# A two-layer graph convolution: the first twelve gathered chunks stand in tiles that the weights and row vectors take later

## The chip, the cores and the metric

The kernel runs on one core of one Trainium2 chip. The time is the device time of one execution, in microseconds (us); less is better. Three runs of the kernel before gave a median of 2044.03 us. Beside them one execution was profiled.

## What is computed

There are N = 6250 nodes with D = 512 values each and E = 100000 edges (src, dst), sorted by dst. All is in float32. A layer norm with a ReLU goes first, then two Chebyshev graph convolutions with a layer norm and a leaky ReLU between them, and at the end x is added:

```python
def _cheb_norm(src, dst, n):
    deg = segment_sum(ones(E), src, n)
    dinv = where(deg > 0, rsqrt(maximum(deg, 1.0)), 0.0)
    return -dinv[src] * dinv[dst]
def _cheb_conv(x, src, dst, norm, W0, W1, b):
    tx1 = segment_sum(x[src] * norm[:, None], dst, N)
    return x @ W0 + tx1 @ W1 + b

h = maximum(layernorm(x), 0.0)
g = _cheb_conv(h, src, dst, norm, W1_0, W1_1, b1)
g = layer_norm(g, gamma, beta)
g = where(g >= 0, g, 0.01 * g)
out = x + _cheb_conv(g, src, dst, norm, W2_0, W2_1, b2)
```

## The kernel before

**Chunks.** The sorted edges are cut into 782 chunks of 128 edges. For a chunk, one indirect DMA on GpSimd's queue gathers the 128 rows that its src name, 2 KB each, into one slot of 128 partitions x 512 values (256 KB). TensorE then multiplies the chunk by a selection matrix (`sel`, one column for each of 32 neighbouring dst) and adds it up into the rows of the nodes. Three chunks make a unit and four units a group: group 0 has chunks 0 to 2, group 1 chunks 3 to 14, group 2 chunks 15 to 26, and so on, 66 groups in each layer. `sums` (L621) does the matmuls of one group.

**Slots.** `places` is one tile with 63 slots. Slots 14 to 62 first hold the 49 blocks of x (128 nodes each). From these the normed table `tab[0]` is made and written to DRAM, and a slot that has been written out is taken by a gather. The last eight slots later hold layer 1's weights, so R = 55 slots are in turn for chunks: chunk t of layer 0 stands in slot t modulo 55 (`zr`), and chunk t can be gathered only when chunk t - 55 has been summed. `gather_to` issues the gathers of a group in order, ahead of the group's work, up to chunk 3 * unit[g] + 55.

**Raw chunks.** `tab[0]` is not complete when the first gathers are wanted. So the first RAW = 64 chunks of layer 0 are gathered from x itself ("raw"). Their norm is made good later: `find` and `look_up` fetch, four chunks at a time, the scale and shift of each gathered row by small matmuls (L477, L492), VectorE steps (L480, L495, L498, L501) and one ScalarE activation for each chunk (L503, a ReLU with scale and shift). Chunks from RAW on come from `tab[0]`, whose rows carry dinv in a further column, and `scale` (L610) multiplies the selection by it.

**First stage.** The first 14 raw chunks go into the slots that never held x. While VectorE builds one-hot matrices for the degrees (L340, 25 rounds), `make_table` norms blocks of x in place (L311), SyncE writes them to `tab[0]` (L312), and `gather_raw` (L236) gathers raw chunks into the slots that come free. The last entry for `tab[0]` is the column of dinv for its first 31 blocks (L393), elements of four bytes.

**Main loop.** `usual_path` writes out the order of TensorE, GpSimd and SyncE by hand: on each of them instructions run in written order, and one that waits holds all behind it. ScalarE's and VectorE's order is left to a scheduler. For each group g: gathers, look-ups, then for the blocks of nodes that are complete `turn` (own rows of h transposed, sums placed, L651), then `sums`, look-ups, and the dense products with the layer's weights `w_sb` (L532) and the layer norm. Block 0 is complete with group 2, so its products come in group 3.

**Weights and row vectors.** `w_sb` is two tiles of four 128 x 512 parts (1 MB each) for layer 0's W1_1 and W1_0. `bias1`, `bias2`, `gam` and `bet` are tiles of 128 x 512; each gets its vector as one row on partition 0 (L204), and `widen` (L798, L799) spreads it over all partitions by a matmul with ones and a VectorE copy. In the kernel before, `load_rest(1)` loads the row vectors in the first stage, `load_rest(3)` stands ahead of the main loop and loads the weights, and `widen` runs behind the sums of group 1. SyncE's written order of the first stage and that of the main loop are two chains that may be merged; in the trace the two weight loads (L201) stand among the first stage's table writes.

Of the kernel before, what the change touches and what calls it, by code (L numbers as in the profile page):

```python
# [12 lines left out]
OP = mybir.AluOpType  # L13
# [6 lines left out]
P = 128  # L20
# [4 lines left out]
Q = 32  # L25
NQ = P // Q
STEP = 3
DRIFT = 32
RE = 14
RAW = 64  # L30
PAD = 16
# [11 lines left out]
def gnn_kernel(  # L43
# [34 lines left out]
    N, D = x.shape  # L78
# [5 lines left out]
    KD = D // P  # L84
    NC = -(-E // P)
# [12 lines left out]
    def dup(ap, n):  # L98
# [4 lines left out]
    zero_row = (NB - LATE) * P  # L103
# [90 lines left out]
    def load_rest(k):  # L194
        if k < 3:
            load_x(*groups[6 + k])
        if k == 2:
            nc.sync.dma_start(tab[1][zero_row : zero_row + 1, :], places[P - 1 : P, RE + NB - 1, :D])
        if k == 3:
            for t, w in zip(w_sb, (W1_1, W1_0)):  # L200
                nc.sync.dma_start(t, w.rearrange("(k p) d -> p k d", p=P))  # L201
# [32 lines left out]
    def gather_raw(lo, hi):  # L234
        for t in range(lo, min(hi, R)):
            nc.gpsimd.indirect_dma_start(  # L236
                out=places[:, t, :D], out_offset=None, in_=x,
                in_offset=bass.IndirectOffsetOnAxis(ap=sidx[:, t : t + 1], axis=0))

    gather_raw(0, RE)  # L240

# [63 lines left out]
    def make_table(i0, n):  # L305

        for lo in range(i0, i0 + n, 2):
            hi = min(lo + 2, i0 + n)
            for i in range(lo, hi):
                v = places[:, RE + i, :D]  # L310
                nc.scalar.activation(v, v, AF.Relu, bias=nb_all[:, i : i + 1], scale=rs_all[:, i : i + 1])  # L311
# [96 lines left out]
def usual_path(tc, have):  # L408
    nc = tc.nc
    (x, out, tab, h_tab, ndinv, sidx, dlx, iota_r, w_sb, W2_1, W2_0, w_late, ident, eps, ones, first, nodes_ps, node_of, minus,  # L410
     unsorted, dinv, sdinv, bias1, bias2, gam, bet, unseen, unit, N, E, D, NB, NC, NU, NS, KD, rows, places, R,
     load_rest, sc, pick, src_lo, src_hi, eidx, e_src, zero_row, p_id) = (
        have[n] for n in ("x out tab h_tab ndinv sidx dlx iota_r w_sb W2_1 W2_0 w_late ident eps ones first nodes_ps node_of "
                          "minus unsorted dinv sdinv bias1 bias2 gam bet unseen unit N E D NB NC NU NS KD rows places "
                          "R load_rest sc pick src_lo src_hi eidx e_src zero_row p_id").split())
    AHEAD = 2
# [10 lines left out]
    with ExitStack() as es:  # L427
        pool = es.enter_context(tc.tile_pool(name="main", bufs=2))
        psum = es.enter_context(tc.tile_pool(name="main_ps", bufs=2, space=bass.MemoryType.PSUM))
        es.enter_context(tc.manual_schedule(engines={PE, POOL, SP}))  # L430
        is_lo, found, looked, gathered = [], 0, 0, R
        behind, behind_rows, summed = {}, {}, {}
# [4 lines left out]
        def zr(layer, t):  # L437
            return places[:, (layer * NC + t) % R, :D]

        def gather_to(layer, end):  # L440
            nonlocal gathered
            for t in range(gathered, min(end, NC)):
                own_scale = layer == 0 and t >= RAW
                nc.gpsimd.indirect_dma_start(  # L444
                    out=places[:, t % R, :] if own_scale else zr(layer, t), out_offset=None,
                    in_=x if layer == 0 and t < RAW else tab[layer],
                    in_offset=bass.IndirectOffsetOnAxis(
                        ap=lidx[:, t - SHIFTED : t - SHIFTED + 1] if layer and t >= SHIFTED else sidx[:, t : t + 1], axis=0))
            gathered = max(gathered, min(end, NC))
# [149 lines left out]
        def scale(sel, chunk, of=(0, NQ)):  # L599

            at = chunk[0][0]
            start = chunk[of[0]][0]
            end = chunk[min(of[1], len(chunk)) - 1][-1] + 1
            if end <= RAW:
                return
            each = sel.rearrange("p q s e -> p (q s) e")
            cut = sorted({start, end} | {t for t in range(start, end) if t % R == 0})
            for lo, hi in zip(cut, cut[1:]):
                v = each[:, lo - at : hi - at, :]
                last = nc.vector.tensor_tensor(  # L610
                    v, v, places[:, lo % R : lo % R + hi - lo, D : D + 1].to_broadcast([P, hi - lo, Q]), op=OP.mult)
            return last
# [173 lines left out]
        find("ps")  # L786
        load_rest(3)
        for i in range(AHEAD):
# [12 lines left out]
        for layer in range(2):  # L801
# [5 lines left out]
            for g in range(NS):  # L807
# [408 lines left out]
```

## Time and profile before

| | |
|---|---|
| median of 3 runs | 2044.03 us (2043.89 to 2047.14) |
| the profiled execution | 2042.93 us, of which its span is 2041.0 us |
| mean granted TensorE clock | 0.916 |
| TensorE busy | 1678.5 us (82%) |
| GpSimd busy | 1506.2 us (74%), 1564 gathers among its instructions |
| VectorE, ScalarE busy | 703.4 us (34%), 406.3 us (20%) |
| moved by DMA | 527.46 MB, mean 258 GB/s |

In the rows of the profile PE is TensorE, DVE VectorE, ACT ScalarE, POOL GpSimd, SPq SyncE's queue. A row in order of time has the start, the duration, the engine, the line, the operation, and in brackets the idle time before it and what ended that. A row of a stretch has for PE, PE's weight loads, DVE, ACT and POOL the busy time and the number of instructions, then the granted clock, the share of the DMA engines and GB/s. A group's row has its count, the busy time and the mean ns of one, and the engine's idle time ahead of its members. TensorE's busy time is not TensorE at its peak, since matmuls are pipelined.

### The profile page before, as it was taken

What the parts mean: (1) busy time and instruction counts of PE and PEld (TensorE: products, weight loads), DVE (VectorE), ACT (ScalarE), POOL (GpSimd) and SP (SyncE); (2) the same over time, 40 slices, a digit from 0 to 9 for tenths busy, and PEclk for the clock granted to TensorE, in tenths of its full rate; (3) what the DMA queues carried; (4) which work ended last, traced back from release to release, by engine and by line L of the source; (5) the groups of instructions that cost most, each with busy time, mean ns of one, the idle gap of its engine ahead of it and who ended that gap; (6) DMA issues with size and microseconds to landing.
All of it is one profiled execution on the core that took longest, in us unless ns stands there. A gap on an engine that the chain in (4) does not pass through costs nothing.

```text
span 2041.0 us, 19914 instructions
## 1 busy us (share of the span) xinstructions
PE 1678.5 (82%) x6838; PEld 662.6 (32%) x6838; DVE 703.4 (34%) x1483; ACT 406.3 (20%) x740; POOL 1506.2 (74%) x1578
## 2 busy tenths in 40 slices
PE   5579997778787767877889888888888888888887
PEld 4444432223333222333333332323332223333332
DVE  7975443232453333443462212122121212212221
ACT  7794221111211111221210101001010001011110
POOL 4677777777777777777777777777777777777774
PEclk9879998889988888988999988999998999999999
DMA  9998888888888888888887888887788888878875
GB/s 338 377 313 255 277 263 248 258 243 262 279 276 256 254 249 252 263 260 260 248 258 234 251 251 251 246 253 246 245 257 251 245 248 256 246 247 256 271 236 157
DMA packets 189414, 527.46 MB, mean 258 GB/s; under 512 B 34550, under 2 KB 36112, under 8 KB 189304
## 3 DMA queue, kind: packets, MB, share of 16 engines
q0 software_dynamic: 125120, 415.98, 68.0%
q1 hardware_dynamic: 64184, 110.12, 15.0%
q8 instruction: 56, 0.92, 0.2%
q14 instruction: 54, 0.44, 0.1%
HBM read 474.31 MB, written 51.66 MB: 258 GB/s over the span
## 4 chain that ended last, share of the span: by engine, by line
PE 42%; DMA 27%; POOL 14%; issue 11%; DVE 6%; ACT 1%; POOLq 0%; DVEq 0%; ACTq 0%; SPq 0%
DMA places<-tab,sidx 21%; PE u_ps L532 16%; POOL places L444 14%; PE ps L621 12%; PE an_ps L651 7%; DMA places<-tab,lidx 6%; PE hT_ps L711 1%; PE hT_ps L520 1%; DVE hi L340 1%; DVE lo L340 1%; PE hT_ps L492 1%; DVE st L671 0%; DVE sel L610 0%; PE both_ps L354 0%; DVE st L385 0%
## 5 line engine op out<-in xcount | busy, mean ns | idle before, releaser
L444 POOL DMA_INDIRECT places<-tab,sidx x1206 | 1145.0, 949 | 372.6 <-issue 266.2
L621 PE MATMUL ps<-places,sel 128*32 128x512 f32 x3128 | 531.6, 688 | 153.6 <-DMA places<-tab,sidx 84.9
L651 PE MATMUL an_ps<-agg,there 128*128 128x512 f32 (+1 forms) x580 | 281.6, 618 | 102.6 <-ACT agg L631 98.1
L444 POOL DMA_INDIRECT places<-tab,lidx x270 | 255.3, 945 | 82.3 <-issue 60.3
L621 PEld LDWEIGHTS ps<-places,sel 128*32 128x32 f32 x3128 | 106.3, 119 | 548.1 <-issue 196.5
L571 DVE TENSOR_TENSOR sel<-dlx,nodes_ps 128x384 f32<-128x384 f32 (+3 forms) x134 | 72.3, 541 | 424.8 <-PE ps L621 424.6
L631 ACT ACTIVATE agg<-ps 128x512 f32<-128x512 f32 (+1 forms) x132 | 78.4, 594 | 576.0 <-PE ps L621 553.6
L532 PE MATMUL u_ps<-w,hT 128*128 128x512 f32 (+1 forms) x392 | 178.7, 599 | 13.1 <-ACT hT L522 13.1
L651 PEld LDWEIGHTS an_ps<-agg,there 128*128 128x128 f32 (+1 forms) x580 | 108.9, 197 | 227.4 <-ACT agg L631 117.0
L532 PE MATMUL u_ps<-w,aT 128*128 128x512 f32 (+1 forms) x392 | 178.4, 598 | 2.5 <-DVE aT L713 2.5
L532 PE MATMUL u_ps<-places,hT 128*128 128x512 f32 (+1 forms) x392 | 176.9, 594 | 2.2 <-ACT hT L522 2.2
L532 PE MATMUL u_ps<-places,aT 128*128 128x512 f32 (+1 forms) x392 | 176.6, 593 | 1.5 <-DVE aT L713 1.5
L610 DVE TENSOR_TENSOR sel<-sel,places 128x384 f32<-128x384 f32 (+11 forms) x73 | 35.3, 485 | 375.1 <-DMA places<-tab,sidx 367.6
L662 DVE TENSOR_TENSOR u_ps<-u_ps,bias 128x512 f32<-128x512 f32 x46 | 32.2, 700 | 286.3 <-PE u_ps L532 286.3
L522 ACT ACTIVATE hT<-hT_ps 128x512 f32<-128x512 f32 (+1 forms) x98 | 58.2, 594 | 277.3 <-PE hT_ps L520 276.7
L639 DVE TENSOR_SCALAR there<-iota_r,node_of 128x128 f32<-128x128 f32 (+1 forms) x290 | 86.5, 301 | 60.9 <-PE an_ps L651 58.3
L704 ACT ACTIVATE an<-an_ps,ndinv 128x512 f32<-128x512 f32 (+1 forms) x98 | 67.1, 684 | 201.7 <-PE an_ps L651 201.4
L674 ACT ACTIVATE sd<-mv,eps 128x1 f32<-128x1 f32 (+1 forms) x49 | 14.4, 294 | 464.3 <-DVE mv L672 464.3
L236 POOL DMA_INDIRECT places<-in_x_dram,sidx x55 | 70.3, 1278 | 46.6 <-ACT junk L291 10.9
L532 PEld LDWEIGHTS u_ps<-w,aT 128*128 128x128 f32 (+1 forms) x392 | 72.5, 191 | 85.7 <-issue 79.4
L532 PEld LDWEIGHTS u_ps<-places,aT 128*128 128x128 f32 (+1 forms) x392 | 72.1, 190 | 83.1 <-issue 80.5
L532 PEld LDWEIGHTS u_ps<-w,hT 128*128 128x128 f32 (+1 forms) x392 | 71.3, 192 | 85.4 <-issue 71.7
(166 smaller groups left out, 1255.1 us busy)
## 6 DMA issues: line engine op xcount, KB each, us to landing
places<-tab,sidx POOLq DMA_INDIRECT x1206, 3.9
h_tab<-g SPq DMA_DIRECT2D x48, 256.0 KB, 5.8
xt<-in_x_dram SPq DMA_DIRECT2D x48, 256.0 KB, 5.1
out_dram<-t SPq DMA_DIRECT2D x48, 256.0 KB, 3.7
h<-tab SPq DMA_DIRECT2D x46, 256.0 KB, 5.0
tab<-t SPq DMA_DIRECT2D x46, 256.0 KB, 4.0
h<-h_tab SPq DMA_DIRECT2D x46, 256.0 KB, 4.5
tab<-places SPq DMA_DIRECT2D x22, 528.0 KB, 10.1
```

The lines of the kernel that those rows point to most:

```text
L236: nc.gpsimd.indirect_dma_start(out=places[:, t, :D], out_offset=None, in_=x, in_offset=bass.IndirectOffsetOnAxis(ap=sidx[:, t : t + 1], ax ...
L340: nc.vector.tensor_tensor(t, s[:, g * 2 * GJ : (g + 1) * 2 * GJ].rearrange("p (j s) -> p j s", s=2)[:, :, None, :] .to_broadcast([EP, GJ, ...
L444: nc.gpsimd.indirect_dma_start(out=places[:, t % R, :] if own_scale else zr(layer, t), out_offset=None, in_=x if layer == 0 and t < RAW el ...
L522: nc.scalar.activation(hT[:, :, :r], ps[:, :, :r], AF.Copy)
L532: nc.tensor.matmul(u_ps[:r], hT[:, kc, :r], w[:, kc, :], start=(start and kc == 0), stop=(stop and kc == KD - 1))
L571: nc.vector.tensor_tensor(sel[:, q : q + k, :w, :], of, node[:, q : q + k, None, :].to_broadcast([P, k, w, Q]), op=OP.is_equal)
L610: last = nc.vector.tensor_tensor(v, v, places[:, lo % R : lo % R + hi - lo, D : D + 1].to_broadcast([P, hi - lo, Q]), op=OP.mult)
L621: nc.tensor.matmul(ps[q * Q : (q + 1) * Q, :], sel[:, q, s, :], zr(layer, chunk[q][s]), start=(s == 0), stop=(s == len(chunk[q]) - 1 and ( ...
L631: nc.scalar.activation(agg[g][: n * Q], ps[: n * Q], AF.Copy)
L639: behind[1] = nc.vector.tensor_scalar(t[:m, :r], iota_r[:m, :r], node_of[:m, g : g + 1], -(1.0 + i * P), op0=OP.subtract, op1=OP.is_equal)
L651: nc.tensor.matmul(placed[i][:r], t[:m, :r], agg[g][:m, :], start=(g == inside[i][0]), stop=(g == inside[i][-1]))
L704: nc.scalar.activation(an[:r], placed.pop(i)[:r], AF.Copy, scale=ndinv[:r, i : i + 1])
```

## The change

Twelve slots more are found in tiles that lie empty at the start: the eight parts of `w_sb` and the four tiles of the row vectors (`lent`, X = 12). Chunks 0 to 11 are gathered there, straight behind each other at the start, and the 14 free slots of `places` take chunks 12 to 25. All further raw gathers move up by twelve chunks. A chunk t from 12 on stands in slot (t - 12) modulo 55. RAW grows from 64 to 76, so three more groups of four chunks are looked up, and `scale` begins with chunk 76. The weights and the row vectors are loaded by `load_rest(3)` behind the sums of group 1, which end the use of the lent tiles, and `widen` moves from behind group 1's sums to behind group 2's. The bound of `gather_to` (3 * unit[g] + 55) stays as it was.

```diff
-RAW = 64
+RAW = 76
...
+    lent = [t[:, k, :] for t in w_sb for k in range(KD)] + [bias1, bias2, gam, bet]
+    X = len(lent)
...
     def load_rest(k):
         if k == 3:
             for t, w in zip(w_sb, (W1_1, W1_0)):
                 nc.sync.dma_start(t, w.rearrange("(k p) d -> p k d", p=P))
-        if k == 1:
             for t, v in ((bias1, b1), (bias2, b2), (gam, gamma), (bet, beta)):
                 nc.sync.dma_start(t[0:1], dup(v, 1))
...
     def gather_raw(lo, hi):
-        for t in range(lo, min(hi, R)):
+        for t in range(lo, min(hi, X + R)):
             nc.gpsimd.indirect_dma_start(
-                out=places[:, t, :D], out_offset=None, in_=x,
+                out=lent[t] if t < X else places[:, t - X, :D], out_offset=None, in_=x,
...
-    gather_raw(0, RE)
+    gather_raw(0, X + RE)
...
-            gather_raw(RE + lo, RE + hi)
+            gather_raw(X + RE + lo, X + RE + hi)
...
-        is_lo, found, looked, gathered = [], 0, 0, R
+        is_lo, found, looked, gathered = [], 0, 0, X + R
...
         def zr(layer, t):
-            return places[:, (layer * NC + t) % R, :D]
+            k = layer * NC + t
+            return lent[k] if k < X else places[:, (k - X) % R, :D]
...
-            cut = sorted({start, end} | {t for t in range(start, end) if t % R == 0})
+            cut = sorted({start, end} | {t for t in range(start, end) if (t - X) % R == 0})
...
         find("ps")
         find("ps")
-        load_rest(3)
         for i in range(AHEAD):
             load(0, i)
...
                 sums(layer, g, sel, chunk, count_late(sel, chunk) if layer == 1 else None, of)
                 if layer == 0 and g == 1:
+                    assert STEP * unit[g + 1] >= X
+                    load_rest(3)
+                if layer == 0 and g == 2:
                     widen()
```

More of the change, by code (lines that the diff above doesn't have):

```diff
@@ L411, in usual_path @@
      unsorted, dinv, sdinv, bias1, bias2, gam, bet, unseen, unit, N, E, D, NB, NC, NU, NS, KD, rows, places, R,
-     load_rest, sc, pick, src_lo, src_hi, eidx, e_src, zero_row, p_id) = (
+     load_rest, sc, pick, src_lo, src_hi, eidx, e_src, zero_row, p_id, lent, X) = (
         have[n] for n in ("x out tab h_tab ndinv sidx dlx iota_r w_sb W2_1 W2_0 w_late ident eps ones first nodes_ps node_of "
                           "minus unsorted dinv sdinv bias1 bias2 gam bet unseen unit N E D NB NC NU NS KD rows places "
-                          "R load_rest sc pick src_lo src_hi eidx e_src zero_row p_id").split())
+                          "R load_rest sc pick src_lo src_hi eidx e_src zero_row p_id lent X").split())
     AHEAD = 2
@@ L444, in gather_to @@
                 nc.gpsimd.indirect_dma_start(
-                    out=places[:, t % R, :] if own_scale else zr(layer, t), out_offset=None,
+                    out=places[:, (t - X) % R, :] if own_scale else zr(layer, t), out_offset=None,
                     in_=x if layer == 0 and t < RAW else tab[layer],
```

3 lines of the change are left out of this document (2 added, 1 removed).

## The prediction

> **What bounds the kernel now.** I read the page first (span, busy shares, groups), then busy time by stretch, then GpSimd's and TensorE's instructions in order of time between 8 and 205 us, last SyncE's issues. The page's span, and the group that issues most gathers:
>
> ```profile
> span 2041.0 us, 19914 instructions
> L444 POOL DMA_INDIRECT places<-tab,sidx x1206 | 1145.0, 949 | 372.6 <-issue 266.2
> L621 PE MATMUL ps<-places,sel 128*32 128x512 f32 x3128 | 531.6, 688 | 153.6 <-DMA places<-tab,sidx 84.9
> ```
>
> One gather takes GpSimd 0.949 us and about 0.3 us pass before the next (372.6 over 1206). The sums (L621) mostly wait for gathers when they wait. Busy time by stretch, the columns and one stretch of 200 us:
>
> ```profile
> core 0: us, PE busy (x) PEld busy (x) DVE busy (x) ACT busy (x) POOL busy (x), PEclk, DMA share, GB/s
> 1200.00:1400.00 200.00, 172.79 (x620) 61.41 (x619) 40.68 (x88) 20.62 (x33) 151.26 (x161) 0.93 0.81 250
> ```
>
> 161 gathers in 200 us are one every 1.25 us without a pause, while TensorE has 14% to spare: the queue of gathers sets the pace. GpSimd in order of time (start, duration, and in brackets what it waited for):
>
> ```profile
> 29.19 2.54 POOL L236 DMA_INDIRECT places<-in_x_dram,sidx  x1 [0.30 <-issue]
> 41.69 1.38 POOL L236 DMA_INDIRECT places<-in_x_dram,sidx  x1 [9.96 <-ACT junk L291]
> ...
> 52.74 1.98 POOL L236 DMA_INDIRECT places<-in_x_dram,sidx  x1 [8.42 <-ACT junk L295]
> ...
> 86.24 1.45 POOL L236 DMA_INDIRECT places<-in_x_dram,sidx  x1 [8.34 <-ACT places L311]
> ...
> 121.41 0.95 POOL L444 DMA_INDIRECT places<-in_x_dram,sidx  x1 [0.30 <-DMA places<-in_x_dram,sidx]
> ...
> 134.82 0.94 POOL L444 DMA_INDIRECT places<-tab,sidx  x1 [2.42 <-ACT places L503]
> ...
> 142.34 0.95 POOL L444 DMA_INDIRECT places<-tab,sidx  x1 [0.30 <-issue]
> ...
> 157.37 0.95 POOL L444 DMA_INDIRECT places<-tab,sidx  x1 [0.30 <-DMA places<-tab,sidx]
> ...
> 172.38 0.94 POOL L444 DMA_INDIRECT places<-tab,sidx  x1 [0.30 <-ACT agg L631]
> ...
> 187.39 0.95 POOL L444 DMA_INDIRECT places<-tab,sidx  x1 [0.30 <-issue]
> ```
>
> Counted along the queue these are chunks 13, 14, 16, 28, 55, 64, 70, 82, 94 and 106. Up to 86.24 the queue stands idle three times, 26.7 us in all; behind 134.82 each row shows the 0.30 between two gathers and no more. So twelve gathers taken out of the paced stretch are worth at most 12 x 1.25 = 15.0 us, if the queue may run on.
>
> It may run on only where a slot is free. Chunk n takes the slot of chunk n - 55, before (n modulo 55) and after ((n - 12) modulo 55) alike, so chunks 70, 82, 94 and 106 wait for the sums of groups 2, 3, 4 and 5. Busy time in four stretches (columns as above), then TensorE in order of time, the sums (L621) of groups 1 to 5, with the spreading of the row vectors (L798) behind group 1's:
>
> ```profile
> 120.00:140.00 20.00, 18.74 (x101) 10.57 (x101) 15.54 (x34) 17.40 (x27) 13.45 (x15) 0.75 1.08 295
> 140.00:160.00 20.00, 17.75 (x114) 9.77 (x107) 11.02 (x24) 15.66 (x24) 15.13 (x17) 1.00 0.79 230
> 160.00:180.00 20.00, 19.49 (x92) 9.25 (x95) 11.37 (x24) 11.80 (x18) 15.13 (x17) 1.00 0.85 254
> 180.00:200.00 20.00, 20.00 (x104) 8.02 (x100) 11.05 (x26) 5.66 (x11) 15.12 (x17) 1.00 0.88 272
> ```
>
> ```profile
> 121.95 3.50 PE L621 MATMUL ps<-places,sel 128*32 128x512 f32 x24
> 125.38 1.12 PE L798 MATMUL u_ps<-bias,ident 1*128 1x512 f32 x2
> ...
> 128.68 1.02 PE L798 MATMUL u_ps<-bias,ident 1*128 1x512 f32 x2
> ...
> 132.04 2.03 PE L492 MATMUL hT_ps<-sc,xt 128*128 128x98 f32 x8 [0.23 <-DVE an L498]
> ...
> 137.11 4.28 PE L621 MATMUL ps<-places,sel 128*32 128x512 f32 x24
> ...
> 143.12 1.13 PE L492 MATMUL hT_ps<-sc,xt 128*128 128x98 f32 x8 [0.44 <-DVE an L498]
> 144.09 0.39 PE L477 MATMUL hT_ps<-src_lo,pick 128*128 128x128 bf16 x4
> ...
> 150.67 2.78 PE L621 MATMUL ps<-places,sel 128*32 128x512 f32 x24
> ...
> 155.73 3.60 PE L532 MATMUL u_ps<-w,hT 128*128 128x512 f32 x8
> ...
> 168.44 2.78 PE L621 MATMUL ps<-places,sel 128*32 128x512 f32 x24
> ...
> 179.52 2.78 PE L621 MATMUL ps<-places,sel 128*32 128x512 f32 x24
> ```
>
> The sums end at 141.39, 153.45, 171.22 and 182.30; the gathers into their slots start at 142.34, 157.37, 172.38 and 187.39. The slack is 0.95, 3.9, 1.2 and 5.1 us. TensorE is busy 18 to 20 of each 20 us there, so a queue that comes 15 us earlier finds the slots taken: of the 15.0 us it can keep about one.
>
> **The change part by part.** *Twelve more raw gathers at the start.* They stand behind the first 14. GpSimd's gathers of the first stage, grouped between 20 and 86 us:
>
> ```profile
> L236 POOL DMA_INDIRECT places<-in_x_dram,sidx x20 | 34.9, 1745 | 24.0 <-ACT junk L291 10.9 <-ACT junk L295 9.0 <-issue 3.5
> ```
>
> At 1.745 + 0.30 us each they take 24.6 us there, and the idle time above is 26.7, so the queue has caught up near 86 us. Behind them stand all later raw gathers, for which nobody waits so early. Gathers 67 to 69 then need group 1's sums (125.45), and number 70 waits for group 2's, with everything behind it on GpSimd. Their 12 x 256 KB = 3.1 MB join the first stage and the weights' 2.1 MB leave it, a net 1 MB; I take nothing for it (its price is under the rivals).
>
> *Three more groups of look-ups (76 chunks, not 64).* The one extra finding ahead of group 4's sums costs TensorE 0.39 us: 0.4. The other steps come after these sums: two look-ups before group 5's at 1.13 each, their wait of 0.44 once, a finding of 0.39: 3.1 us. Twelve more activations on ScalarE and three more sets on VectorE lie beside TensorE: between 160 and 200 us VectorE is busy 11 of each 20 us and ScalarE 12 and 6 (rows above), so they are taken at nothing. Without that cover they would cost 12 x 0.80 = 9.6 us of ScalarE (the row of L503 among the rows below).
>
> *The spreading moves from behind group 1's sums to behind group 2's.* It lasts from 125.45 to 129.70, 4.25 us. Group 2's sums then end at 141.39 - 4.25 = 137.1, and what follows is where it was, if the row vectors have landed by 137.1. That is the new wait: TensorE goes in written order, so behind the spreading stand group 3's look-ups, its sums and through them the slots for chunk 82 and on.
>
> *The weights and row vectors are loaded late.* They are issued on SyncE's queue once group 1's sums are over (125.45), behind the loads of h:
>
> ```profile
> L503 ACT ACTIVATE places<-places,ac 128x512 f32<-128x512 f32 x64 | 46.0, 801 | 10.8 <-DVE ac L501 10.8
> 27.20 1.58 SPq L201 DMA_DIRECT2D w<-in_L_gnn_W_dram  x1
> 69.12 0.39 SPq L201 DMA_DIRECT2D w<-in_L_gnn_W_dram  x1
> 114.37 1.67 SPq L393 DMA_DIRECT2D tab<-dinv  x1
> 116.21 15.68 SPq L509 DMA_DIRECT2D h<-tab  x1
> places<-in_L_gnn_W_dram SPq DMA_DIRECT2D x2, 1024.0 KB, 17.2
> 50.00:80.00 30.00, 17.66 (x167) 15.57 (x166) 29.98 (x26) 28.07 (x67) 21.65 (x12) 0.92 1.04 383
> ```
>
> Before, the weights were issued at 27.20 and 69.12 and hidden. Now SyncE is held: the column of dinv (31 x 128 elements of four bytes) is issued at 114.37, and the load of h behind it keeps the queue until 131.9. So the weights are issued between 125.5 and 132.4. Layer 1's two weights, the same 2 x 1 MB in the middle of the gathers, landed after 17.2 us; at the 383 GB/s that all transfers together reach between 50 and 80 us, 2.1 MB take 5.5 us. That gives 131 to 149.6 for the row vectors, which are issued last. I take 139.5: an issue at 130, because no gather competes with the dinv column while the queue waits for group 2, and 9.5 us, nearer to the fast end, because GpSimd issues only three gathers between 125.5 and 137. The products that need the weights begin at 155.73, so the weights themselves cost nothing unless the vectors land after that.
>
> **The sum.** With W the time at which the spreading can start (137.1 or the vectors' landing, whichever is later), group 4's sums end at W + 4.25 + (171.22 - 141.39) + 0.4 = W + 34.5, and chunk 94 is issued 0.3 later, at W + 34.8; before it was 172.38. The shift is W - 137.6. With W = 139.5 it is +1.9 us, at W = 137.1 it is -0.5. Group 5's sums follow after 11.1 + 3.1 = 14.2 us, less than the 12 x 1.25 = 15.0 of the queue, so from chunk 94 on the pace holds again and carries the shift to the end, through both layers. On the profiled execution (2042.93 us, 1.9 more than its span, 1.1 under the median of the runs) that is 2044.8; on the median of 2044.03 it is 2045.9.
>
> **The rivals.** *A: the vectors land late.* Then TensorE stands behind the spreading. It decides from W = 141.7, a shift of 4.1. For it: h took 15.68 us to be issued, and gathers 70 on start at 137 and share the DMA engines. With W = 146 the shift is 8.4 and the time 2052.4; at 149.6 it is 2056. Against it: the quiet queue between 129 and 137. [...]
>
> *B: the gathers keep their lead.* If the slots came free in time, the time would be 2044.0 - 15.0 = 2029. For it: the queue is the bound wherever it never rests. Against it: the slacks of 0.95 and 1.2. A part of it is open: two look-ups of the same form took 2.03 and 1.13 us, and sums 4.28 and 2.78, so 3 to 4 us lie in the slower pace between 129 and 141 (granted clock 0.75 between 120 and 140 us, 1.00 in the next 20); without it, and with the vectors early, the shift is -4, the time 2040.
>
> *C: the first stage gets longer.* DMA is at a share of 1.04 between 50 and 80 us; a net 1 MB at 383 GB/s is 2.7 us, and if that delays the last tables the shift is 1.9 + 2.7 = 4.6, the time 2048.6. Against it: VectorE, not DMA, is busy 29.98 of 30 us there.
>
> **How the numbers follow.** My forecast (shift -1 to +4, 2043 to 2048) has 0.47, A 0.33, B in whole or part 0.12, C 0.08. The range leaves out most of B and the far end of A: 2040 to 2054. About 0.2%, 4.1 us, is what a measurement of this kernel can tell from no change: faster is B, 0.12; slower is A and most of C, 0.40; the same 0.48.
>
> **What would show it.** Right: chunk 26's gather near 55 us, the queue idle before chunk 70 until group 2's sums end near 137, again no pause after chunk 94 at about 174, and L798 behind group 2's sums with a wait of a few us for the row vectors. A wait there over 5 us means A. No idle time of GpSimd before 150 us and chunk 94 before 165 would make the argument of the slots wrong; sums of group 1 ending after 128 would mean C.

## The result and the profile after

The changed kernel takes 2060.63 us (median of 6 runs, 2058.12 to 2063.12), the kernel before 2044.34 us beside it (6 runs, 2039.21 to 2047.14): a ratio of 1.008 with a 95% interval of 1.0068 to 1.0092, 16.3 us more. The profiled execution of after took 2063.12 us, 1.8 more than its span, which is 20.3 us longer than that of before. It is the longest of the six, 2.5 us over their median, so shifts read from its profile come out a little larger than the 16.3 us. The page of the profile after, its span and its two costliest groups:

```profile
span 2061.3 us, 20007 instructions
L447 POOL DMA_INDIRECT places<-tab,sidx x1194 | 1134.1, 950 | 394.8 <-issue 264.4
L625 PE MATMUL ps<-places,sel 128*32 128x512 f32 x3104 | 520.6, 676 | 148.1 <-DMA places<-tab,sidx 85.2
```

The twelve gathers have left the paced group (1206 before) at the same 0.95 us each, and GpSimd's idle time ahead of the group has grown from 372.6 to 394.8 us. The sums' 3104 matmuls of 676 ns each lie in 520.6 us of busy time: they overlap. Where that idle time lies is seen in GpSimd's instructions of after in order of time (start, duration, in brackets the idle time before and what ended it); these are chunks 69, 70, 81, 82, 94 and 106:

```profile
127.10 0.94 POOL L447 DMA_INDIRECT places<-in_x_dram,sidx  x1 [0.30 <-issue]
130.87 1.10 POOL L447 DMA_INDIRECT places<-in_x_dram,sidx  x1 [2.83 <-PE ps L625]
...
145.27 0.95 POOL L447 DMA_INDIRECT places<-tab,sidx  x1 [0.30 <-issue]
172.82 0.94 POOL L447 DMA_INDIRECT places<-tab,sidx  x1 [26.60 <-PE ps L625]
...
191.45 0.94 POOL L447 DMA_INDIRECT places<-tab,sidx  x1 [3.93 <-PE ps L625]
...
206.45 0.95 POOL L447 DMA_INDIRECT places<-tab,sidx  x1 [0.30 <-PE ps L625]
```

Up to chunk 81 the queue is ahead of before. Then it stands still for 26.6 us until TensorE comes to group 3's sums: chunk 82 takes the slot of their first chunk, and chunk 83 goes behind it, at 174.07. Chunk 94 starts 19.1 us later than before (191.45 against 172.38), and this shift stays to the end: the span is 20.3 us longer.

What TensorE did meanwhile (after, in order of time; L625 are the sums of groups 2, 3 and 4, L801 the spreading, L495 a look-up, L655 the placing of rows):

```profile
130.94 2.76 PE L625 MATMUL ps<-places,sel 128*32 128x512 f32 x18 [0.33 <-ACT places L506]
148.37 2.07 PE L801 MATMUL u_ps<-bias,ident 1*128 1x512 f32 x2 [14.67 <-DMA bias<-in_L_gnn_b_dram]
...
155.50 2.03 PE L495 MATMUL hT_ps<-sc,xt 128*128 128x98 f32 x8
...
165.21 5.78 PE L655 MATMUL an_ps<-agg,there 32*128 32x512 f32 x6
170.92 2.88 PE L625 MATMUL ps<-places,sel 128*32 128x512 f32 x24
...
189.66 2.78 PE L625 MATMUL ps<-places,sel 128*32 128x512 f32 x24
```

It waited 14.67 us for the row vectors. From the spreading on its instructions are slow: a look-up takes 2.03 us, in the full clock 1.13. Chunks 82 and 94 start 1.9 and 1.8 us behind the start of the sums that they wait for and ahead of their end, so a slot is free before the whole group has been summed. The busy time by stretch shows the granted clock (the column behind POOL):

```profile
120.00:140.00 20.00, 12.12 (x96) 6.64 (x96) 13.30 (x32) 19.12 (x29) 12.99 (x14) 0.93 1.04 287
140.00:160.00 20.00, 11.39 (x28) 6.38 (x29) 4.46 (x7) 0.71 (x1) 4.73 (x5) 0.50 0.47 183
160.00:180.00 20.00, 18.40 (x80) 9.29 (x79) 8.46 (x19) 12.66 (x19) 5.65 (x6) 0.72 0.26 70
180.00:200.00 20.00, 17.99 (x100) 9.75 (x99) 12.71 (x28) 11.91 (x18) 12.31 (x14) 1.00 0.73 216
```

The clock is at half from 137.0 to 171.2 us, 34.1 us at a stretch; before it was so from 130.0 to 140.2. Last, why the row vectors came late, in SyncE's issues of after:

```profile
113.58 1.67 SPq L395 DMA_DIRECT2D tab<-dinv  x1
115.81 17.19 SPq L512 DMA_DIRECT2D h<-tab  x2
133.09 0.96 SPq L204 DMA_DIRECT2D w<-in_L_gnn_W_dram  x2
134.15 0.70 SPq L206 DMA_DIRECT2D bias<-in_L_gnn_b_dram  x2
134.95 0.29 SPq L206 DMA_DIRECT2D gam<-in_L_gnn_gamma_dram  x1
```

Group 1's sums were over near 124.8, but the two loads of h kept the queue until 133.0. The weights are issued then, the vectors behind them.

So two things came together: a late landing, and a slow clock that was still there when the landing was over. The first is the prediction's rival A. The second nobody had forecast, and most of the experiments are about it.

### The profile page after: what moved, and what is told of

Its sections match the earlier page's. It is cut to its first block, busy times and chain, and to the rows that moved or that the text cites. A ratio compares the mean times of both kernels' runs of the same rounds, so it can differ in the third digit from the quotient of the medians.

```text
span 2061.3 us, 20007 instructions
## 1 busy us (share of the span) xinstructions
PE 1690.2 (82%) x6874; PEld 672.1 (33%) x6874; DVE 706.4 (34%) x1493; ACT 415.6 (20%) x752; POOL 1521.4 (74%) x1578
## 4 chain that ended last, share of the span: by engine, by line
PE 46%; DMA 26%; POOL 12%; issue 9%; DVE 6%; ACT 1%; DVEq 0%; POOLq 0%; ACTq 0%; SPq 0%
DMA places<-tab,sidx 18%; PE u_ps L535 18%; PE ps L625 14%; POOL places L447 12%; PE an_ps L655 9%; DMA places<-tab,lidx 6%; PE hT_ps L523 2%; PE hT_ps L715 2%; DVE hi L342 1%; DVE lo L342 1%; PE hT_ps L495 1%; DMA bias<-in_L_gnn_b_dram 1%; PE both_ps L356 1%; DVE sel L614 1%; DVE st L675 0%
## 5 line engine op out<-in xcount | busy, mean ns | idle before, releaser
L447 POOL DMA_INDIRECT places<-tab,sidx x1194 | 1134.1, 950 | 394.8 <-issue 264.4
L625 PE MATMUL ps<-places,sel 128*32 128x512 f32 x3104 | 520.6, 676 | 148.1 <-DMA places<-tab,sidx 85.2
L655 PE MATMUL an_ps<-agg,there 128*128 128x512 f32 (+1 forms) x580 | 286.0, 627 | 103.6 <-ACT agg L635 99.6
L625 PEld LDWEIGHTS ps<-places,sel 128*32 128x32 f32 x3104 | 103.5, 118 | 534.8 <-issue 188.6
L655 PEld LDWEIGHTS an_ps<-agg,there 128*128 128x128 f32 (+1 forms) x580 | 110.3, 199 | 231.6 <-ACT agg L635 117.4
L614 DVE TENSOR_TENSOR sel<-sel,places 128x384 f32<-128x384 f32 (+11 forms) x71 | 34.5, 488 | 366.5 <-DMA places<-tab,sidx 360.0
L535 PEld LDWEIGHTS u_ps<-places,hT 128*128 128x128 f32 (+1 forms) x392 | 71.0, 191 | 73.8 <-issue 71.0
```

What stands on the lines that cost most here:

```text
L447: nc.gpsimd.indirect_dma_start(out=places[:, (t - X) % R, :] if own_scale else zr(layer, t), out_offset=None, in_=x if layer == 0 and t < ...
L535: nc.tensor.matmul(u_ps[:r], hT[:, kc, :r], w[:, kc, :], start=(start and kc == 0), stop=(stop and kc == KD - 1))
L614: last = nc.vector.tensor_tensor(v, v, places[:, k : k + hi - lo, D : D + 1].to_broadcast([P, hi - lo, Q]), op=OP.mult)
L625: nc.tensor.matmul(ps[q * Q : (q + 1) * Q, :], sel[:, q, s, :], zr(layer, chunk[q][s]), start=(s == 0), stop=(s == len(chunk[q]) - 1 and ( ...
L655: nc.tensor.matmul(placed[i][:r], t[:m, :r], agg[g][:m, :], start=(g == inside[i][0]), stop=(g == inside[i][-1]))
```

## The experiments

Each time is a median, with the ratio to the kernel before on the same chip and its 95% interval. "Slow" is the stretch of half clock around the spreading. Where two are given, one of them lies elsewhere: the first in f3 (from 147.6 us) and in g1 (151.6), the second in g2 (195.9), and so does the one of i3 (195.6); there TensorE had waits of 1.3 to 2.8 us. 94 is the start of chunk 94's gather in the profiled execution (172.38 in before, 191.45 in after; on the chips of the last five rows before takes 2039.3 us, and its chunk 94 probably starts some 3 us earlier: see i1 below).

| kernel | us | before | ratio | spreading | slow, us | 94 |
|---|---|---|---|---|---|---|
| e1 rows first | 2050.60 | 2043.39 | 1.0037 [1.0027, 1.0048] | 138.02 | 23.9 | 181.63 |
| e2 weights lent | 2041.53 | 2043.39 | 0.9992 [0.9980, 1.0004] | 123.99 | 10.2 | 169.46 |
| e3 vectors lent | 2048.37 | 2043.39 | 1.0025 [1.0013, 1.0037] | 136.05 | 20.5 | 178.38 |
| e4 late, none lent | 2056.51 | 2043.39 | 1.0064 [1.0043, 1.0085] | 145.36 | 30.7 | 187.58 |
| f1 vectors early | 2044.02 | 2042.64 | 1.0008 [0.9998, 1.0017] | 133.49 | 17.1 | 173.97 |
| f2 20 fillers | 2059.17 | 2042.64 | 1.0090 [1.0073, 1.0106] | 151.27 | 13.7 | 190.27 |
| f3 sums first | 2041.29 | 2042.64 | 0.9991 [0.9976, 1.0006] | behind group 4 | 6.8 and 6.8 | 163.93 |
| f4 sums first, none lent | 2042.12 | 2042.64 | 0.9998 [0.9987, 1.0009] | behind group 4 | 6.8 | 174.41 |
| g1 parked | 2036.94 | 2043.55 | 0.9970 [0.9960, 0.9979] | behind group 6 | 3.4 and 3.4 | 165.43 |
| g2 parked, 8 lent | 2037.03 | 2043.55 | 0.9972 [0.9963, 0.9982] | behind group 6 | 3.4 and 6.8 | 164.64 |
| g3 15 fillers | 2059.06 | 2043.55 | 1.0076 [1.0061, 1.0090] | 147.20 | 20.5 | 189.20 |
| h3 full rows | 2037.43 | 2039.27 | 0.9991 [0.9981, 1.0001] | 132.91 | none | 166.31 |
| h4 behind group 3 | 2036.11 | 2039.27 | 0.9982 [0.9973, 0.9992] | 143.80 | 6.8 | 168.20 |
| i1 before, full rows | 2039.48 | 2039.34 | 1.0002 [0.9991, 1.0012] | behind group 1 | none | 169.61 |
| i2 late, full rows | 2048.87 | 2039.34 | 1.0042 [1.0027, 1.0056] | 146.13 | 13.7 | 181.50 |
| i3 parked, full rows | 2032.91 | 2039.34 | 0.9963 [0.9950, 0.9975] | behind group 6 | 3.4 | 161.98 |

**Is it the late load?** e1 issues the four vectors ahead of the weights:

```diff
         if k == 3:
-            for t, w in zip(w_sb, (W1_1, W1_0)): ...
             for t, v in ((bias1, b1), (bias2, b2), (gam, gamma), (bet, beta)): ...
+            for t, w in zip(w_sb, (W1_1, W1_0)): ...
```

> The changed kernel with one thing swapped: behind group 1's sums SyncE issues the four row vectors (8 KB) first and the weights (2 MB) behind them. Theory 1 (the row vectors land late because 2 MB of weights stand ahead of them in SyncE's queue, and TensorE stands still before the spreading): the vectors land at 135 to 138 us, the wait before L801 shrinks from 14.7 us to under 4, chunk 94 is gathered at 171 to 175 us as in the kernel before, and the time is 2042 to 2048 us, 0.998 to 1.002 of the kernel before. Rival 2 (the twelve extra gathers and three more groups of look-ups cost the time, in the first stage or on TensorE): nothing changes, about 2060 us, 1.008. Rival 3 (the four-byte column of dinv and the loads of h hold the vectors, not the weights): the wait shrinks by less than a third, 2055 to 2060 us.

e2 lends the eight weight tiles only; the vectors are loaded and spread where they were. e3 lends the four vector tiles only; the weights are loaded where they were. (The main lines; the calls of `load_rest` and `widen` are moved to match.)

```diff
# e2
-RAW = 76
+RAW = 72
-    lent = [... for k in range(KD)] + [bias1, bias2, gam, bet]
+    lent = [... for k in range(KD)]
+        if k == 1:
             for t, v in ((bias1, b1), ...):
# e3
-RAW = 76
+RAW = 68
+    lent = [bias1, bias2, gam, bet]
```

> One part of the change alone: only the eight parts of the weights' tiles are lent (eight extra chunks, 72 raw), the row vectors are loaded in the first stage and spread behind group 1's sums as before; the weights are loaded late. Theory 1: no wait for row vectors; the weights land near 149 us, ahead of the first products at about 156; 2041 to 2047 us, 0.998 to 1.001 of the kernel before. Rival 2 (extra gathers and look-ups cost): two thirds of the loss, about 2055 us. If the late weights themselves hold the first products: a wait of L535 for a DMA and a time between the two.

> The other part alone: only the four tiles of the row vectors are lent (four extra chunks, 68 raw); the weights are loaded early as in the kernel before, the row vectors behind group 1's sums, spread behind group 2's. Theory 1: without the weights ahead of them the vectors land at 134 to 138 us, the wait before the spreading is under 4 us, and the time 2042 to 2048 us. Rival 2: a third of the loss, about 2050 us. Rival 3 (SyncE's queue is held by the column of dinv and h): a wait of 8 us and more, 2052 us and more.

e4 is the kernel before with nothing but the loads and the spreading moved to where the change has them:

```diff
-        load_rest(3)
...
                 if layer == 0 and g == 1:
+                    load_rest(3)
+                if layer == 0 and g == 2:
                     widen()
```

> The kernel before with only the loads moved: nothing is lent, 64 raw chunks, but the weights and then the row vectors are loaded behind group 1's sums and the vectors are spread behind group 2's, as in the changed kernel. Theory 1: the whole loss appears without any lending: a wait of 8 to 15 us before L798 and 2055 to 2063 us, 1.006 to 1.009 of the kernel before. Rival 2: no loss, 2043 to 2047 us.

The spreading in e1 and in e2, in TensorE's order of time:

```profile
138.02 2.07 PE L801 MATMUL u_ps<-bias,ident 1*128 1x512 f32 x2 [5.10 <-DMA bias<-in_L_gnn_b_dram]
```

```profile
123.99 1.12 PE L802 MATMUL u_ps<-bias,ident 1*128 1x512 f32 x2
```

With the vectors in front the wait falls from 14.67 to 5.10 us, and the loss from 16.3 to 7.2. With them early it is gone, and so is the loss. e4, in which no gather is moved at all, loses 13.1 us. e3, with a wait of 2.69 us, loses 5.0. So the late vectors make the loss; the lending alone makes none that is clear of noise (f1 below, which lends eleven tiles with the vectors early, is 1.4 us over before). But in e1 the spreading starts at 138.02, less than half a microsecond behind the 137.6 at which the forecast's formula gives no shift, and chunk 94 still comes 9.25 us late, not at the expected 171 to 175. The wait isn't all.

**Is it the pause of TensorE?** The theory after e1 to e4 was that a pause lets the clock fall and so stretches what follows. f1 has no pause: eleven tiles are lent, and the vectors come early as four rows of the twelfth:

```diff
-    lent = [...] + [bias1, bias2, gam, bet]
+    lent = [...] + [bias1, bias2, gam]
+        if k == 1:
+            for j, v in enumerate((b1, gamma, b2, beta)):
+                nc.sync.dma_start(bet[j : j + 1], dup(v, 1))
...
-                nc.tensor.matmul(ps, ident[0:1, 0:1].to_broadcast([1, P]), t[0:1, :], ...)
+                nc.tensor.matmul(ps, ident[0:4, j : j + 1].to_broadcast([4, P]), bet[0:4], ...)
```

> The changed kernel without the late row vectors: eleven tiles are lent (the eight parts of the weights, bias1, bias2, gam), all four vectors are loaded in the first stage as four rows of the twelfth tile, and the spreading stays behind group 2's sums (76 raw chunks). So TensorE has no wait there. Theory 1a (TensorE's pause ahead of the spreading is also what stretches the slow clock behind it, from 10 us in the kernel before to 20 to 34 us): the slow stretch that starts between 128 and 138 us is 10 to 14 us long, chunk 94 is gathered at 169 to 173 us, and the time is 2038 to 2045 us. Rival 1b (the place of the spreading, or the full-speed run of TensorE ahead of it, stretches the slow clock, wait or none): the slow stretch stays at 20 us or more, chunk 94 comes at 177 to 181 us, 2048 to 2052 us. Rival 2 (more gathers and look-ups cost): 2055 us and more.

f2 and g3 are the changed kernel with matmuls of full size on other data in the pause (20, then 15; their results are not used):

```diff
                 if layer == 0 and g == 2:
+                    fill = psum.tile([P, D], F32, name="u_ps")
+                    for _ in range(20):
+                        nc.tensor.matmul(fill, ident, dlx[:, :D], start=True, stop=True)
                     widen()
```

> The changed kernel with 20 more matmuls of 128x512 ahead of the spreading, whose results nobody reads: TensorE is busy for 9 to 15 us of its 14.7 us of waiting, and the wait for the row vectors itself is untouched. Theory 1a (the pause stretches the slow clock): the slow stretch falls from 34 to 10 to 17 us, chunk 94 comes at 182 to 186 us, not 191, and the time is 2051 to 2056 us. Rival 1b (the pause has nothing to do with the clock): the slow stretch is as long or longer, 2058 to 2068 us.

> The changed kernel with 15 matmuls of unread results ahead of the spreading (20 of them ended at 151.3 us, 3 us after the vectors had come; 15 at 0.87 us each end near 147). Theory 1a (TensorE's pause stretches the slow clock): W stays at 148 to 149 us, the slow stretch is 10 to 14 us, chunk 94 is gathered at 185 to 188 us and the time is 2054 to 2057 us. Rival 1b: a slow stretch of 20 us and more and 2059 to 2062 us, as in the changed kernel.

In g3, in TensorE's order of time, the added matmuls, the spreading and the first look-up:

```profile
132.70 13.14 PE L851 MATMUL u_ps<-dlx,ident 128*128 128x512 f32 x30
147.20 1.33 PE L801 MATMUL u_ps<-bias,ident 1*128 1x512 f32 x2 [1.35 <-DMA bias<-in_L_gnn_b_dram]
...
153.57 2.03 PE L495 MATMUL hT_ps<-sc,xt 128*128 128x98 f32 x8
```

The theory fell as the only cause. f1 had no pause and 17.1 us of half clock. g3 held the clock through its pause (1.35 us of it were left) and had 20.5 us from 148.0 on, just behind the spreading's start. f2's began at 156.5, right behind the spreading's end at 155.2; its 13.7 us are inside the 10 to 17 that the theory had for it, but its time is not. Its added matmuls ended only at 151.3, later than the vectors land in after, so g3 is the cleaner of the two. What f1, f2 and g3 share is the spreading ahead of the slow stretch.

**Is it the few rows, or what stands behind them?** The spreading contracts one row (`1*128` in the profile; four in f1), look-ups and sums 128 (`128*128`, `128*32`). h3 is f1 with all rows, the other 124 zeros; h4 is f1 with the four rows kept and the spreading put behind group 3's sums, where one look-up and then products follow.

```diff
# h3
+    nc.gpsimd.memset(bet, 0.0)
-  ident[0:4, j : j + 1].to_broadcast([4, P]), bet[0:4]
+  ident[:, j : j + 1].to_broadcast([P, P]), bet
# h4
-                if layer == 0 and g == 2:
+                if layer == 0 and g == 3:
                     widen()
```

Their first runs, h1 and h2, fell on a chip on which the kernel before took 2458 us and TensorE stood still for 5 to 11 us at a time; their 2471.13 and 2467.52 us tell nothing on this question, and the same kernels ran again on another chip as h3 and h4.

> The same kernel as h1, run again on another chip because on the one of h1 the kernel before itself took 2458 us. Theory 'few rows count as rest': with 128 rows contracted in the spreading there is no slow clock from 137 us on, or only 3.4 us of it; group 4's sums end near 165 us instead of 173, chunk 94 is issued near 166 and the time is 2036 to 2040 us. Rival 'what stands behind the spreading decides': the slow clock comes as before, 14 to 20 us of it from about 137 us on, chunk 94 near 174 and the time 2042 to 2046 us.

> The same kernel as h2, run again on another chip for the same reason. Theory 'what stands behind the spreading decides': behind group 2's sums the look-ups alone may still bring a slow stretch, of 3 to 7 us; behind the spreading (now after group 3's sums) the products are dense and bring at most 3.4 to 7 us; group 4's sums end near 166 to 169 us, and the time is 2038 to 2042 us. Rival 'few rows count as rest': the slow stretch moves with the spreading, begins within 3 us of it and lasts 14 to 20 us; group 4's sums end near 173 us and the time is 2042 to 2046 us.

TensorE in f1, in order of time: the spreading, the first look-up behind it, the placing, group 3's sums and group 4's:

```profile
133.49 3.88 PE L802 MATMUL u_ps<-bet,ident 4*128 4x512 f32 x8
137.30 1.89 PE L496 MATMUL hT_ps<-sc,xt 128*128 128x98 f32 x8
...
146.87 5.78 PE L656 MATMUL an_ps<-agg,there 32*128 32x512 f32 x6
152.58 3.73 PE L626 MATMUL ps<-places,sel 128*32 128x512 f32 x24
...
172.18 2.78 PE L626 MATMUL ps<-places,sel 128*32 128x512 f32 x24
```

And the same instructions in h3, whose spreading lasts as long:

```profile
132.91 3.89 PE L803 MATMUL u_ps<-bet,ident 128*128 128x512 f32 x8
136.64 1.03 PE L497 MATMUL hT_ps<-sc,xt 128*128 128x98 f32 x8
...
142.91 3.04 PE L657 MATMUL an_ps<-agg,there 32*128 32x512 f32 x6
145.87 2.78 PE L627 MATMUL ps<-places,sel 128*32 128x512 f32 x24
...
164.51 2.78 PE L627 MATMUL ps<-places,sel 128*32 128x512 f32 x24
```

The busy time between 140 and 160 us, first of f1, then of h3:

```profile
140.00:160.00 20.00, 18.40 (x78) 9.78 (x79) 9.38 (x21) 11.30 (x17) 8.51 (x9) 0.64 0.61 220
```

```profile
140.00:160.00 20.00, 17.57 (x102) 9.97 (x103) 11.35 (x25) 15.24 (x23) 14.21 (x15) 1.00 0.84 281
```

With all rows the clock stays at 1.00 (in each 20 us from 120 to 180), look-ups and placing take half as long, and group 4's sums start 7.7 us earlier, though the order of the instructions is the same. In this place the few rows set off the slow clock; f1 against h3 shows it, and i1 against before shows it once more below. h4 agrees: there the stretch has moved with the spreading (it begins at 147.2, behind the spreading's start at 143.80), and behind group 2's sums, where the same look-ups follow without a spreading, there is none. It is shorter, 6.8 us, so what stands behind has a say in its length, as the theory in h4's expectation had it. That holds over all runs: a few-row spreading with three look-ups behind it is followed by 10.2 to 20.5 us of half clock where TensorE had no long wait ahead (before, e2, f1, f2, g3), one with products at once or nearly so by 3.4 to 6.8 (h4, f3, f4, g1, g2). The 2037.43 us of h3 are inside the 2036 to 2040 that were expected of it, but so is before on that chip (2039.27): beside it the gain is 1.8 us, with an interval that just takes in nothing. h4, few rows and all, gains 3.2 us, and its interval doesn't. Measured against i1's chunk 94 (169.61) rather than before's, h3's lead there is 3.3 us.

**How much does each part make in the changed kernel itself?** i2 is the changed kernel, late loads and all, with the vectors as four rows of a tile of zeros and the spreading over 128 rows; i1 has the same four rows and the same spreading in the kernel before, with the vectors loaded early and the zeros written by GpSimd. The main lines of i2:

```diff
+            nc.vector.memset(bet, 0.0)
+            for j, v in enumerate((b1, gamma, b2, beta)):
+                nc.sync.dma_start(bet[j : j + 1], dup(v, 1))
...
+                nc.tensor.matmul(ps, ident[:, j : j + 1].to_broadcast([P, P]), bet, ...)
```

> The kernel before, only the four row vectors lie as four rows of one tile of zeros and the spreading contracts all its 128 rows. Theory 'few rows count as rest': the slow clock from 130.0 to 140.2 us of before is gone, group 2's sums end 3 to 4 us earlier, near 137.5 us. But the gathers of before stand in their queue there (each 0.3 us behind the one before it), so chunk 94 stays at 171 to 173 us and the time at 2039 to 2045 us, the same as before. Rival 'the gathers of before already wait for TensorE': chunk 94 comes 3 us earlier and the time falls by 3 us.

> The changed kernel with its late loads, only the row vectors are loaded as four rows of one tile of zeros and the spreading contracts all its 128 rows. The row vectors still land near 147 to 149 us. Theory 'few rows count as rest, and so does a pause': the slow clock still begins near 137 us, in the pause, but ends within 3 to 7 us behind the spreading's start, near 152 to 155 us, not at 171 us; group 4's sums end 34.5 to 37 us behind the spreading's start, chunk 94 near 184 us, 12 us later than in the kernel before, and the time is 2052 to 2056 us. Rival 'the landing alone makes the loss': the time stays at 2058 to 2062 us.

TensorE in i2: the spreading, the first look-up, the sums of groups 3 and 4:

```profile
146.13 5.86 PE L802 MATMUL u_ps<-bet,ident 128*128 128x512 f32 x8 [13.14 <-DMA bet<-in_L_gnn_beta_dram]
151.83 1.03 PE L496 MATMUL hT_ps<-sc,xt 128*128 128x98 f32 x8
...
161.06 2.78 PE L626 MATMUL ps<-places,sel 128*32 128x512 f32 x24
...
179.70 2.78 PE L626 MATMUL ps<-places,sel 128*32 128x512 f32 x24
```

The wait is nearly as long, and the clock falls in it, at 136.9. But it is full again at 150.5, 4.4 us behind the spreading's start; in after it took 22.8 (148.4 to 171.2). Group 4's sums end 36.4 us behind the spreading's start, in after 44.1. The loss falls from 16.3 us to 9.5 by the medians, on another chip (8.6 by the ratio). So somewhat more than half of the loss is the landing, and the rest, about 7 us, the clock behind one-row matmuls. i2's time came out lower than expected (2052 to 2056), with chunk 94 at 181.5, not 184; against i1, on the same chip, chunk 94 is 11.9 us and the time 9.4 us later (i2's profiled execution is the longest of its five, 3.8 us over their median). In i1 the slow 10.2 us go, too, group 2's sums start at 132.32 instead of 137.11, and nothing comes of it: there the gathers stand in their own queue, and the slow clock was hidden. Chunk 94 of i1 starts at 169.61, 2.8 us ahead of before's profile, but the time is that of before on that chip; i1's queue was that much earlier by chunk 55 (119.7 against 121.4) and chunk 64 (131.8 against 134.8), where the clock had no part in it or hardly any. Starts are therefore compared across chips only to about 3 us.

**A version that beats both.** If chunk 82 and 94 wait for sums, the sums should stand ahead of what nobody waits for. f3 (on f1) puts the spreading behind group 4's sums and the second halves of blocks behind the sums in groups 3 to 6; f4 does so with nothing lent. g1 (on f1) and g2 (on e2) hold all of that back until group 6's sums are over; i3 is g1 with 128 rows. In all five the spreading also writes another PSUM tile. The main lines of g1:

```diff
# g1
+                if layer == 0 and 2 < g <= 6:
+                    parked, left = parked + left, []
-                if layer == 0 and g == 2:
+                if layer == 0 and g == 6:
                     widen()
+                    for k, aT in parked:
+                        second(layer, k, aT)
```

> Eleven tiles lent and the vectors early, as in the run above, and in groups 3 to 6 TensorE does the sums of a group before the second half of the finished block's products; the spreading moves behind group 4's sums. Theory 1 (slots, freed by the sums, hold the queue of gathers): with sums 3 and 4 some 4 and 8 us earlier, chunk 94 comes at 161 to 168 us, and the lead stays to the end: 2032 to 2040 us, 0.994 to 0.998 of the kernel before. Rival (the queue is held by something else, or TensorE gives the lead back later): 2041 us and more.

> The same order of TensorE without lending: the kernel before (64 raw chunks, weights and vectors early), spreading behind group 4's sums and the second halves behind the sums in groups 3 to 6. Theory 1: here the table, complete at about 134.8 us, holds chunk 64, so earlier slots are worth at most about a microsecond: 2041 to 2046 us. Rival (the order alone is what gains): as fast as the kernel with eleven lent tiles.

> Eleven lent tiles, vectors early (as in f1), and the second halves of blocks 0 and 1 and the spreading all wait until group 6's sums are done, so that TensorE frees slots before it does products. Theory 1 (the lead of the gathers lasts where every group's sums come before its slots are wanted; in f3 it was lost at group 5's): chunk 94 at 162 to 166 us, chunk 106 at 177 to 182, chunk 130 at 207 to 213, and the lead of 6 to 9 us reaches the end: 2033 to 2038 us, 0.995 to 0.998 of the kernel before. Rival (TensorE's backlog takes the lead back, at group 7 or later, since all the work still has to be done): a pause of GpSimd before chunk 118 to 154 and 2040 us and more.

> The same order with eight lent tiles only (the weights', 72 raw chunks; row vectors loaded in the first stage into their own tiles). Theory 1: chunk 72, the first from the table, is held until the table is complete near 134 us, then as in the run above: chunk 94 at 162 to 166 us, 2033 to 2038 us. Rival: as above, 2040 us and more.

> The kernel in which the second halves of blocks 0 and 1 and the spreading are parked until after group 6's sums, with all 128 rows contracted in the spreading. Theory: the slow clock behind the spreading there (3.4 us from 189.2 us on) goes, and with it at most 2 us; chunk 94 stays near 165.4 us; the time is 2035 to 2038 us. Rival: the gathers set the pace by then, nothing changes, 2037 us.

GpSimd's longest wait behind chunk 55 in f4 (this is chunk 64) and in f3 (chunk 106):

```profile
136.83 0.94 POOL L444 DMA_INDIRECT places<-tab,sidx  x1 [5.42 <-ACT places L503]
```

```profile
186.42 0.94 POOL L448 DMA_INDIRECT places<-tab,sidx  x1 [7.79 <-ACT places L507]
```

Without lending the order is worth nothing: chunk 64, the first to read the scaled table, is held until 136.83, and from there the queue runs without a rest, one gather every 1.25 us, to chunk 94 at 174.41. (The row names a step of ScalarE; that it is the table that chunk 64 waits for is a reading.) In f3 chunk 94 starts 8.5 us earlier than in before's profile, but the work put off by one group falls on group 5's sums: they start at 184.63, and chunk 106 starts 1.8 us behind that, as chunks 82 and 94 do in after, whatever its row names. Held back for longer (g1, g2) the lead lasts: 6.6 and 6.5 us. i3 has chunk 94 at 161.98 and 6.4 us, so the rows add nothing to the time that these runs could tell (its 2032.91 is under the 2035 to 2038 expected, on a chip where before, too, takes some 4 us less than beside g1).

## Why the prediction was wrong

The forecast was 2045.9 us, with 2040 to 2054; the kernel takes 2060.63.

*What bounds the kernel, and the slots: right.* The shift of chunk 94 is carried to the end (19.1 us there, 20.3 in the span). Chunks 70, 82 and 94 wait for sums, named as releaser in GpSimd's rows, and behind 94 the queue doesn't rest. Twelve gathers fewer brought no gain by themselves. Rival B held only once sums were moved ahead of other work, for 3.2 us in h4 and for 6 to 7 of the 15.0 in g1, g2 and i3. One reading was off: I measured the slack to the end of a group's sums, but chunks 70, 82 and 94 of after start 1.3 to 1.9 us behind the start of theirs, so each slack was about 1 us larger than I had it.

*First stage and look-ups: right.* Group 1's sums ended near 124.8, before at 125.45, so rival C was wrong. Chunk 26 started at 60.3, not near 55, and nobody waited for it. The added look-ups were hidden.

*The spreading moved: half right.* I had group 2's sums end at 137.1; they ended at 133.7, since the slow stretch behind the spreading went with it. I had put these 3 to 4 us under rival B as a slower pace between 129 and 141 us with no cause, and did not ask whether the pace would move with the spreading.

*The weights and row vectors are loaded late: this step failed.* "I take 139.5" became 148.4. The issue was at 133.1, not 130, behind h; it is later than my latest bound of 132.4. The landing came 15.3 us behind it, not 9.5, near the slow bound of 17.2 that a row of the same size had given. I took a value near the fast end because GpSimd would issue only three gathers between 125.5 and 137. It issued seven, and seven more before the landing: group 2's sums started at 129.56 and let chunk 70 go at 130.87, not at 137. Between 133.1 and 148.4 the DMA engines moved 5.65 MB at 370 GB/s, close to the 383 that I had counted on, but 3.03 MB of it stood on the queue of the gathers. That the vectors stand behind the 2.1 MB of weights I had in the sum; e1, where they were issued from 133.39 on ahead of the weights and had landed by 138.02, shows what that place costs. No run takes the gathers away, so their part of the 15.3 us is worked out, not shown. By the formula, 148.4 makes a shift of 10.8 us and 2054.8 us, already over the end of the range. That is rival A, to which I gave 0.33.

*"What follows is where it was": this step failed too.* The term W + 34.5 was 44.1 in after, 9.6 us more. It held in h3, where the spreading contracts 128 rows and the clock stays full (34.4), and to 2 us in i2, where the spreading starts in the half clock that the pause has left (36.4). The 9.6 us are half clock: 23 us of it lie behind the spreading's start in after. The sign was to be seen: the clock of 0.75 between 120 and 140 us in before stood just behind the spreading. Chunk 94 started 1.0 us ahead of the sums' end, not 0.3 behind it. With the terms as measured, 10.8 + 9.6 - 1.3 = 19.1 us, the shift of chunk 94 is met.

## What to carry to other kernels

A step that is moved takes its side effects along: ask of each slow stretch in the profile what stood just ahead of it, and expect it at the new place, where it may no longer be hidden (half clock from 130.0 to 140.2 us in before, from 137.0 to 171.2 in after). A small load that someone waits for goes ahead of the large ones on its queue (the wait fell from 14.67 us in after to 5.10 in e1), and is costed by what that queue still holds and, by my estimate, by what else moves meanwhile (3.03 of 5.65 MB in after). Slots freed by an engine that works in written order came no sooner because their users were ready (chunk 82 of after waited 26.6 us); reorder the engine's own work first (chunk 94 at 165.43 in g1, 173.97 in f1). And where TensorE's clock is on the path, write small broadcasts as matmuls over all rows: that was worth about 7 us between after and i2, and nothing in i1 and i3, where gathers set the pace.

## What the runs showed of the hardware

Matmuls that contract one row or four did not keep TensorE's clock up. It fell to half during them or within 1.5 us of their end, for 10.2 to 20.5 us where look-ups followed (before, e2, f1, f2, g3) and 3.4 to 6.8 where products did (h4, f3, f4, g1, g2). With 128 rows, most of them zeros, it stayed full (h3, i1), though a spreading lasts 3.9 us in either form; in i3 one stretch of 3.4 us came 10 us behind the spreading, beside a wait of 2.82 us. Nor did they bring the clock back after a pause: 7.1 us of them did not in after, 128 rows did in 4.4 us (i2). They are not the only cause: in f3 and g1 the clock also fell, for 6.8 and 3.4 us, with none of them ahead, beside waits of 1.3 to 1.6 us. In after and i2 it fell inside the waits of 14.67 and 13.14 us, 3.3 and 3.9 us behind the end of group 2's sums. The stretches named here and in the table, with the 34.1 us of after, last 3.4, 6.8, 10.2, 13.7, 17.1, 20.5, 23.9, 30.7 or 34.1 us, each within 0.1 us of a multiple of 3.4. So a stream of few-row matmuls was followed by half clock as these waits were. Why the look-ups behind them, 128 rows deep and nearly back to back (waits of 0.43 us between them in h3, 0.23 in f1), kept the clock where it was (full in h3, 1.03 to 1.13 us each; half in f1, 1.89 to 2.03) until the next placing and sums, isn't settled.

The first two loads of h held SyncE for 13.8 to 18.4 us in after, e1 to e4, f1 and i2 (17.19 in after, 18.39 in e1, 14.15 in i2), and in these three what stood behind them was issued at 133.09, 133.39 and 129.78.
